# A shorter opening for a two-layer pair kernel: four-step prelude, batches by size, an earlier code exchange on GpSimd, small operations on ScalarE

## The chip, the cores and the metric

The kernel runs on one core of a Trainium2 chip. A core has a matrix engine (TensorE, PE in the profile; its weight loads are listed apart as PEld), a vector engine (VectorE, DVE), a scalar engine (ScalarE, ACT), a general engine (GpSimd, POOL) and a queue engine that issues most transfers (SyncE, SP). Each works through its own list of instructions in order; semaphores order them among each other. Transfers between the chip's memory (HBM) and on-chip memory (SBUF) run on 16 DMA engines. TensorE writes to PSUM, which GpSimd does not read.

The metric is device time in microseconds (us), as the median over runs. The "granted clock" is the share of full speed at which TensorE's clock ran.

## What is computed

The input is x, 384 x 384 x 128 in float32. Two layers follow each other (biases are zeros, scales ones, but the kernel treats them as inputs):

```python
# layer 0
z = layernorm(x)                                   # over the 128 channels
left  = (z @ Wl + bl) * sigmoid(z @ Wlg + blg)     # 384 x 384 x 128
right = (z @ Wr + br) * sigmoid(z @ Wrg + brg)
core  = einsum('ikh,jkh->ijh', left, right)
x = x + sigmoid(x @ Wg + bg) * (layernorm(core) @ Wout + bout)
# layer 1, on the new x
left  = x @ W_left + b_left + x @ W_eq + b_eq
rsum  = sum(x @ W_right + b_right, axis=2)
out   = (left * rsum * sigmoid(x @ W_gate + b_gate)) @ W_out + b_out
return layernorm(out + x)
```

## The kernel before, in words

It works in three phases. Phase 1 makes left and right for all positions and stores them to a scratch tensor, lr_d. Phase 2 multiplies them into core, one channel h at a time (L580). Phase 3 does the rest by rows. The change touches phase 1 alone.

**Chunks, steps, halves.** Phase 1 has 144 chunks (`chunks`). A chunk holds eight rows i for 128 positions k, that is 128 partitions x 8 x 128 numbers, 512 KB. A chunk is two steps, 288 in all; a step (`n, q`) is four rows, and each step has two halves of two rows. In a half, `back` multiplies two 128 x 128 blocks of x by the 128 x 512 weights `wz` (L367, one matmul a row; a float32 matmul leaves two records in the trace), ScalarE takes the sigmoid of one part (L377, tile sg), and VectorE multiplies it with the other part and with the row's scale into tile lr (L379). PSUM has three buffers for `pr`, each holding one half.

**The layernorm is folded in.** `fold` and `weights` put scale and shift of the layernorm into wz and into the shift: three small operations on GpSimd (L181 to L183) on values loaded at the start, four matmuls (L186, L187), two VectorE operations (L194). What stays for each row is a mean-like term `nd`, subtracted from x ahead of the matmul, and a factor `rs`, the reciprocal root, applied after it. For these, VectorE takes statistics of each row (`stats`, bn_stats, L264), then five small operations for a batch of chunks (`powers`, L276 to L280); GpSimd raises to the power -0.5, one operation for each chunk of the batch (`power`, L287, "pow" below); VectorE finishes `nd` by two or three small operations (`centres`, L297, L298, and L300 for the first eight chunks).

**Shift and transposition.** The matmul needs the channels on the partitions. The first eight chunks (PLAIN) are loaded by position; `shift` subtracts nd on GpSimd (L312), and `front` transposes four blocks on TensorE (L327) and copies them back on ScalarE (L328). All later chunks are loaded a second time from a transposed copy (`load_columns`, L135, tile xc). For these, `store_nd` transposes a batch's nd on TensorE (L342), copies it on ScalarE (L344) and stores it to nd_d (L345); `load_shift` loads one row of it per step (L140, tile bc, four buffers); `shift` broadcasts that row over the partitions on GpSimd (L315) and subtracts (L316). The broadcast needs other GpSimd code than the standard one, fetched by a load_library at step 4 (L447; the standard code comes back six steps before the end).

**The order.** The order of each engine's instructions is that of the program (`seq`). Ahead of the main loop a prelude of AHEAD = 6 steps takes statistics, folds the weights and prepares step 0 (`first_step`). In the main loop, step k emits, in this order: one or two pows (two up to k = 40); the shift for step k + 2; `back` for its first half, `centres`, `front` of step k + 1, powers of the next batch, if no batch is under way, and statistics for a later step; then the same for its second half; then the transfers: store_nd, load_columns, load_shift for step k + 6, loads of x (`fetch`), a slice of lr. At k = 4 the shifts run four steps ahead at once, and then comes load_library. Statistics run ahead of the step by a lead that grows by one step a step, from 7 to LEAD = 25. The small weights of the later phases are loaded at k = 4 and combined at k = 20 and 21 (`late_weights`, `late_products`, with a tile m2 of its own).

**Batches.** The first eight chunks are batches of one. Then follow sizes 1, 1, 2, 2, 2, 2, and 4 from there on.

SP's queue carries, in order, the loads of x, of xc and of bc, and the stores of nd and lr; a transfer also waits for the one eight places ahead of it.

Of the kernel before, what the change touches and what calls it, by code (L numbers as in the profile page):

```python
# [8 lines left out]
F32 = mybir.dt.float32  # L9
# [10 lines left out]
def triangle_then_gated_row_kernel(ctx: ExitStack, tc: tile.TileContext, a: dict, out: bass.AP):  # L20
# [59 lines left out]
    with ExitStack() as ctx2:  # L80
# [16 lines left out]
        with tc.tile_pool(name="p1w", bufs=5, side="right") as wp, \  # L97
# [7 lines left out]
            NQ = XR // 4  # L105
            AHEAD, LEAD = 6, 25
            TURN, FETCH = 9, 6
# [3 lines left out]
            batches, at = [(n, n + 1) for n in range(PLAIN)], PLAIN  # L111
            for size in [1, 1, 2, 2, 2, 2] + [4] * len(chunks):
                if at < len(chunks):
                    batches.append((at, min(at + size, len(chunks))))
                    at = batches[-1][1]
# [44 lines left out]
            make_identity(nc, ident)  # L160

            warm = const([P, 1], "warm")
            seq(nc.scalar.activation(warm, mhalf[:, 0:1], AF.Sigmoid))
# [11 lines left out]
            def fold():  # L175
# [4 lines left out]
                busy(1, 1)  # L180
                seq(nc.gpsimd.tensor_tensor(d, b0, g0, ALU.subtract))  # L181
                seq(nc.gpsimd.tensor_tensor(m1, avg, d.to_broadcast([P, P]), ALU.mult))
                seq(nc.gpsimd.tensor_tensor(g0, g0, g0, ALU.add))  # L183

# [38 lines left out]
            def late_weights():  # L223

                m2 = wp.tile([P, C], F32, tag="m2", name="m2", bufs=1)
                seq(nc.vector.tensor_scalar(m2, avg, go, -0.5, ALU.mult, ALU.mult))

                seq(nc.vector.tensor_add(wleft, wleft, weq))
                seq(nc.vector.tensor_add(bleft, bleft, beq))

                seq(nc.vector.tensor_scalar(lns, lns, -1.0, None, ALU.mult))
                return m2
# [29 lines left out]
            def powers(own, lo, hi):  # L266

                if lo == 0:
                    g = XR * (own[1] - own[0])
                    terms[own] += [sp.tile(s, F32, tag=t, name=t, bufs=c)[:, :g] for t, s, c in  # L270
                                   (("mv", [P, 4 * XR, 2], 1),
                                    ("nd", [P, 4 * XR], 2) if own[0] >= PLAIN else ("nd0", [P, XR], PLAIN),
                                    ("rs", [P, 4 * XR], 7) if own[0] >= PLAIN else ("rs0", [P, XR], PLAIN))]
# [17 lines left out]
            def centres(count):  # L291

                for _ in range(count):
# [5 lines left out]
                    if own[0] < PLAIN:  # L299
                        seq(nc.vector.tensor_scalar(nd, nd, 0.5, None, ALU.mult))  # L300
                    centred.add(own)

            centred = set()
            means = []
# [88 lines left out]
            fetch = {0: [4, 5], 1: [6, 7]}  # L393
            for n in range(PLAIN, len(chunks)):
                fetch.setdefault(max(2 + (n - PLAIN) // 2, n - 7, 2 * n - LEAD - 7), []).append(n)
            nds, columns, shifts = {}, {}, {}
# [14 lines left out]
            for k in range(AHEAD):  # L411
# [10 lines left out]
                elif k == 1:  # L422
                    powers((0, 1), 4, XR)
                    power()
                elif k < AHEAD - 1 and k % NQ == 1:
                    powers(batch[k // NQ], 0, XR)
                    power()
                if k == 1:
                    first_step()
                if k == 2:  # L430
                    shift(*steps[1])
            shifted = 2
            powers((2, 3), 0, XR)
            power()
            waiting = batches[AHEAD // NQ:]
            for k, (n, q) in enumerate(steps):
                early = len(means)
                for _ in range(min(len(pows), 1 if k > 40 else 2)):
                    power()
                early = early if k > 40 else len(means)  # L440
                more = 4 if k in (4, len(steps) - 6) else 1
                while shifted < min(len(steps), k + 2 + more):
                    shift(*steps[shifted])
                    shifted += 1
                if more > 1:
                    lib = library_config.all_libraries[10] if k == 4 else library_config.standard
                    seq(nc.gpsimd.load_library(lib))  # L447
                turned = [b for b in batches[PLAIN:] if NQ * b[0] - (TURN if b[0] >= PLAIN + 4 else TURN - 2) == k]
                for half in range(2):
                    if k == 0:  # L450

                        back(n, q, half, (lambda: front(*steps[1])) if half else None)
                    else:
                        back(n, q, half)
                        if half == 0:
                            centres(early)
                        if half == 0 and k + 1 < len(steps):
                            front(*steps[k + 1])
                    if half == 0 and not means and not pows and waiting and 2 * NQ * waiting[0][1] <= given:
                        own = waiting.pop(0)  # L460
                        powers(own, 0, XR * (own[1] - own[0]))
                    stats_to(2 * (k + min(LEAD, AHEAD + k + 1)) + half + 1)
                if q == NQ - 1:
                    del loaded[n], normed[n], columns[n]
                for b in turned:
                    assert b in centred, (k, b, waiting[:1], pows, means)
                    store_nd(b)
                if q == NQ - 1:
# [482 lines left out]
```

## Time and profile before

| | |
|---|---|
| time, median of 3 runs | 3178.05 us (3177.92 to 3178.09) |
| the profiled execution, its own time | 3176.98 us |
| its span | 3175.2 us |
| granted clock, mean | 0.998 |
| TensorE busy | 3144.1 us |
| VectorE, ScalarE, GpSimd busy | 2452.9, 1811.9, 2384.1 us |
| first L367 matmul | 11.91 us |
| first L580 matmul (phase 2) | 1032.43 us |
| read from and written to HBM | 508.14 MB, 286.36 MB |

The span reaches from the first to the last instruction of the one execution that was profiled; its own time is a little longer. Busy time is the time in which an engine executes instructions. In a timeline, a line gives start, duration, engine, source line, operation, output and input tiles, size, and the count of instructions merged; in brackets stands the idle time of the engine ahead of it and what ended it. In the chain of waits, a line gives start, duration, and what was then on the chain that ended last. The phases can be told by their lines: L367 is phase 1, L580 phase 2.

### The profile page before, as it was taken

What the parts mean: (1) busy time and instruction counts of PE and PEld (TensorE: products, weight loads), DVE (VectorE), ACT (ScalarE), POOL (GpSimd) and SP (SyncE); (2) the same over time, 40 slices, a digit from 0 to 9 for tenths busy, and PEclk for the clock granted to TensorE, in tenths of its full rate; (3) what the DMA queues carried; (4) which work ended last, traced back from release to release, by engine and by line L of the source; (5) the groups of instructions that cost most, each with busy time, mean ns of one, the idle gap of its engine ahead of it and who ended that gap; (6) DMA issues with size and microseconds to landing.
All of it is one profiled execution on the core that took longest, in us unless ns stands there. A gap on an engine that the chain in (4) does not pass through costs nothing.

```text
span 3175.2 us, 44349 instructions
## 1 busy us (share of the span) xinstructions
PE 3144.1 (99%) x11344; PEld 1875.8 (59%) x11344; DVE 2452.9 (77%) x7201; ACT 1811.9 (57%) x3793; POOL 2384.1 (75%) x3045
## 2 busy tenths in 40 slices
PE   8999999999999999999999999999999999999998
PEld 3444444444444666666666666677777777777776
DVE  8878888888875555555555788888888888888998
ACT  4444444444444333433433577777777777777776
POOL 5888888888886666666665587787788888888887
PEclk9999999999999999999999999999999999999999
DMA  4787878878782999999999865666666666666552
GB/s 157 289 326 271 329 297 308 315 288 337 272 327 86 266 283 281 285 282 282 284 282 282 302 229 211 216 225 222 218 223 218 224 217 223 219 220 219 209 209 110
DMA packets 474829, 797.41 MB, mean 251 GB/s; under 512 B 21329, under 2 KB 385297, under 8 KB 458194
## 3 DMA queue, kind: packets, MB, share of 16 engines
q1 hardware_dynamic: 473280, 792.61, 72.7%
q8 instruction: 94, 1.54, 0.2%
q10 hardware_dynamic: 1234, 1.77, 0.2%
q14 instruction: 157, 1.29, 0.1%
q0 software_dynamic: 64, 0.20, 0.0%
HBM read 508.14 MB, written 286.36 MB: 250 GB/s over the span
## 4 chain that ended last, share of the span: by engine, by line
PE 95%; POOL 2%; DVE 1%; issue 1%; DMA 1%; ACT 1%; SPq 0%; ACTq 0%; POOLq 0%; DVEq 0%
PE pr L367 28%; PE pc L580 23%; PE py L750 8%; PE pr L721 8%; PE pg L738 8%; PE pl L739 8%; PE pg L690 8%; PE py L751 4%; POOL rs L287 1%; DVE lr L379 1%; POOL xc L316 0%; DVE st L264 0%; DMA xt<-in_x_nat_dram 0%; POOL bc L315 0%; DMA stage<-in_x_nat_dram 0%
## 5 line engine op out<-in xcount | busy, mean ns | idle before, releaser
L367 PE MATMUL pr<-wz,xc 128*128 128x512 f32 x2176 | 939.9, 592 | 5.0 <-ACT sg L377 4.3
L377 ACT ACTIVATE sg<-pr,rs 128x256 f32<-128x256 f32 x1152 | 483.2, 470 | 522.3 <-ACT sg L377 346.4
L580 PE MATMUL pc<-rr,lrh 128*128 128x384 f32 x2304 | 743.3, 486 | 0.3 <-DVE lr L379 0.3
L367 PEld LDWEIGHTS pr<-wz,xc 128*128 128x128 f32 x2176 | 409.8, 190 | 522.7 <-issue 433.6
L379 DVE SCALAR_TENSOR_TENSOR lr<-pr,rs,sg 128x256 f32<-128x256 f32 x1152 | 502.3, 478 | 197.5 <-ACT sg L377 197.5
L580 PEld LDWEIGHTS pc<-rr,lrh 128*128 128x128 f32 x2304 | 452.0, 196 | 291.8 <-issue 1.1
L785 ACT ACTIVATE py<-py,nm,rs 128x128 f32<-128x128 f32 x1149 | 491.8, 429 | 158.2 <-DVE u L743 80.1
L750 PEld LDWEIGHTS py<-wo,u 128*128 128x128 f32 x2304 | 376.6, 191 | 97.5
L591 DVE TENSOR_TENSOR csum<-csum,ct 128x1152 f32<-128x1152 f32 x127 | 176.2, 1387 | 333.8 <-ACT ct L589 333.8
L750 PE MATMUL py<-wo,u 128*128 128x128 f32 x2304 | 402.1, 275 | 0.0
L589 ACT COPY ct<-pc 128x1152 f32<-128x1152 f32 x127 | 142.2, 1119 | 445.2 <-PE pc L580 439.7
L712 POOL TENSOR_TENSOR cs<-ct,rt 128x384 f32<-128x384 f32 x380 | 378.8, 998 | 7.6 <-PE pr L721 4.1
L820 POOL TENSOR_TENSOR yt<-yt,lnb 128x384 f32<-128x384 f32 x380 | 379.7, 1001 | 2.9 <-DVE yt L814 2.6
L316 POOL TENSOR_TENSOR xc<-xc,bc 128x512 f32<-128x512 f32 x272 | 345.2, 1269 | 23.9
L287 POOL TENSOR_TENSOR rs<-nd,mhalf 128x8 f32<-128x8 f32 (+1 forms) x145 | 235.7, 1628 | 157.4 <-ACT ndt L344 107.3
L765 DVE BATCH_NORM_STATS2 st<-py 128x6 f32<-128x128 f32 x1152 | 266.4, 287 | 88.9 <-PE py L751 86.9
L561 POOL COPY rr<-lrh 128x768 f32<-128x768 f32 x128 | 193.7, 1513 | 165.3 <-DMA lrh<-lr_d 154.3
L751 PE MATMUL py<-ident,x1T 128*128 128x128 f32 x1152 | 314.0, 273 | 0.0
L721 PE MATMUL pr<-cs,wc 128*128 128x384 f32 x768 | 313.5, 490 | 0.0
L738 PE MATMUL pg<-x1T,mat_L_conv_W_gate 128*128 128x384 f32 x768 | 310.7, 486 | 0.9 <-ACT g L741 0.9
L690 PE MATMUL pg<-xt,mat_L_conv_Wg 128*128 128x384 f32 x768 | 310.7, 487 | 0.3 <-ACT ct L604 0.2
L739 PE MATMUL pl<-x1T,mat_L_conv_W_left 128*128 128x384 f32 x768 | 310.5, 486 | 0.0
(125 smaller groups left out, 4284.6 us busy)
## 6 DMA issues: line engine op xcount, KB each, us to landing
lr_d<-lr SPq DMA_DIRECT2D x128, 1024.0 KB
lrh<-lr_d SPq DMA_DIRECT2D x128, 640.0 KB
xt<-in_x_row_dram SPq DMA_DIRECT2D x96, 768.0 KB
ct<-core_d SPq DMA_DIRECT2D x95, 768.0 KB
rt<-rstd_d SPq DMA_DIRECT2D x95, 768.0 KB
out_dram<-yt SPq DMA_DIRECT2D x94, 768.0 KB
core_d<-ct SPq DMA_DIRECT2D x125, 576.0 KB
xt<-in_x_nat_dram SPq DMA_DIRECT2D x136, 512.0 KB
```

Of the source, the lines that this page charges most:

```text
L367: seq(nc.tensor.matmul(pr[:, r, :], lhsT=columns[n][:, 4 * q + 2 * half + r, :], rhs=wz, start=True, stop=True))
L377: seq(nc.scalar.activation(sg[r], pr[:, r, 2 * H:], AF.Sigmoid, scale=rs[r]))
L379: seq(nc.vector.scalar_tensor_tensor(t[:, :, c * XR + r0 + r, :], pr[:, r, :2 * H].rearrange("k (h s) -> k h s", s=2), rs[r], sg[r].rearra ...
L580: seq(nc.tensor.matmul(banks[ib], lhsT=t[:, kb, ib * P:(ib + 1) * P, 0], rhs=rr[:, kb], start=(kb == 0), stop=(kb == NB - 1),))
L690: seq(nc.tensor.matmul(pg[:, :N], lhsT=wg0, rhs=r["xT"], start=True, stop=True))
L721: seq(nc.tensor.matmul(pr[:, :N], lhsT=wc, rhs=r["cs"], start=True, stop=True))
L738: seq(nc.tensor.matmul(pg2[:, :N], lhsT=wgate, rhs=r["x1T"], start=True, stop=True))
L739: seq(nc.tensor.matmul(pl[:, :N], lhsT=wleft, rhs=r["x1T"], start=True, stop=True))
L750: seq(nc.tensor.matmul(py[:, s], lhsT=r["u"][:, s], rhs=r["wo"], start=True, stop=False))
L751: seq(nc.tensor.matmul(py[:, s], lhsT=r["x1T"][:, s], rhs=ident, start=False, stop=True, is_transpose=True))
L785: seq(nc.scalar.activation(py[:, s], py[:, s], AF.Identity, bias=bias, scale=scale))
L820: seq(engine.tensor_tensor(yt, yt, lnbb, ALU.add))
```

## The change

It does five things.

- The code exchange of GpSimd (load_library) moves from step 4 to the place right behind the making of the identity matrix; the block of four shifts ahead of it goes.
- The three small operations of `fold` go from GpSimd to ScalarE as activations.
- The prelude has four steps instead of six. The first step's shift stands directly behind the first pow, and other pows and shifts alternate.
- Batches behind the first ten chunks: seven of two, then fours. Up to three batches of one, two of two, and one of four may be under way at once (`free`, `begin`, with buffers of mv by size); one pow a step everywhere. nd has three buffers instead of two; m2 shares the four buffers of bc.
- The lead of the statistics (`goal`) grows by one step a step up to step 12, from 5 to 17, then by one step in three up to 25. Statistics are split evenly over the halves. The loads of x follow `goal`; store_nd comes two steps behind `centres`, or six steps ahead of need at the latest, instead of nine (seven for the first batches).

```diff
-            AHEAD, LEAD = 6, 25
+            AHEAD, LEAD = 4, 25
...
-            for size in [1, 1, 2, 2, 2, 2] + [4] * len(chunks):
+            for size in [1, 1] + [2] * 7 + [4] * len(chunks):
...
             make_identity(nc, ident)
 
+            seq(nc.gpsimd.load_library(library_config.all_libraries[10]))
...
-                seq(nc.gpsimd.tensor_tensor(d, b0, g0, ALU.subtract))
-                seq(nc.gpsimd.tensor_tensor(m1, avg, d.to_broadcast([P, P]), ALU.mult))
-                seq(nc.gpsimd.tensor_tensor(g0, g0, g0, ALU.add))
+                seq(nc.scalar.activation(d, g0, AF.Identity, bias=b0, scale=-1.0))
+                seq(nc.scalar.activation(m1, avg, AF.Copy, scale=d))
+                seq(nc.scalar.activation(g0, g0, AF.Copy, scale=2.0))
...
-                m2 = wp.tile([P, C], F32, tag="m2", name="m2", bufs=1)
+                m2 = bcp.tile([P, 4 * P], F32, tag="bc", name="m2")[:, :C]
...
-                                   (("mv", [P, 4 * XR, 2], 1),
-                                    ("nd", [P, 4 * XR], 2) if own[0] >= PLAIN else ("nd0", [P, XR], PLAIN),
+                                   ((f"mv{g}", [P, g, 2], {XR: 3, 2 * XR: 2}.get(g, 1)),
+                                    ("nd", [P, 4 * XR], 3) if own[0] >= PLAIN else ("nd0", [P, XR], PLAIN),
...
-                    centred.add(own)
-
-            centred = set()
+                    centred[own] = now[0]
+
+            centred, now = {}, [-1]
+
+            def free(own):
+                flying = {p[0] for p in pows} | {p[0] for p in means}
+                size = own[1] - own[0]
+                return sum(o[1] - o[0] == size for o in flying) < {1: 3, 2: 2}.get(size, 1)
+
...
-            for n in range(PLAIN, len(chunks)):
-                fetch.setdefault(max(2 + (n - PLAIN) // 2, n - 7, 2 * n - LEAD - 7), []).append(n)
...
                 elif k == 1:
                     powers((0, 1), 4, XR)
+                    first_step()
                     power()
-                elif k < AHEAD - 1 and k % NQ == 1:
-                    powers(batch[k // NQ], 0, XR)
+                elif k == 2:
+                    shift(*steps[1])
+                else:
+                    powers((1, 2), 0, XR)
                     power()
-                if k == 1:
-                    first_step()
-                if k == 2:
-                    shift(*steps[1])
             shifted = 2
-            powers((2, 3), 0, XR)
-            power()
             waiting = batches[AHEAD // NQ:]
+            turning = batches[PLAIN:]
+
+            def goal(k):
+
+                return 2 * (k + 1 + min(LEAD, 5 + min(k, 12 + (k - 12) // 3))) if k >= 0 else 2 * AHEAD
+
+            for n in range(PLAIN, len(chunks)):
+                k = 2 + (n - PLAIN) // 2
+                while goal(k) < 2 * NQ * (n - 4):
+                    k += 1
+                fetch.setdefault(k, []).append(n)
+
+            def begin(k):
+
+                while waiting and 2 * NQ * waiting[0][1] <= given and free(waiting[0]):
+                    own = waiting.pop(0)
+                    powers(own, 0, XR * (own[1] - own[0]))
+                    if k > 0:
+                        break
+
             for k, (n, q) in enumerate(steps):
+                now[0] = k
                 early = len(means)
-                for _ in range(min(len(pows), 1 if k > 40 else 2)):
+                for _ in range(min(len(pows), 1)):
                     power()
-                early = early if k > 40 else len(means)
-                more = 4 if k in (4, len(steps) - 6) else 1
-                while shifted < min(len(steps), k + 2 + more):
-                    shift(*steps[shifted])
-                    shifted += 1
-                if more > 1:
-                    lib = library_config.all_libraries[10] if k == 4 else library_config.standard
-                    seq(nc.gpsimd.load_library(lib))
-                turned = [b for b in batches[PLAIN:] if NQ * b[0] - (TURN if b[0] >= PLAIN + 4 else TURN - 2) == k]
+                early = early if k > 6 else len(means)
+                if k > 0:
+                    more = 4 if k == len(steps) - 6 else 1
+                    while shifted < min(len(steps), k + 2 + more):
+                        shift(*steps[shifted])
+                        shifted += 1
+                    if more > 1:
+                        seq(nc.gpsimd.load_library(library_config.standard))
...
                         back(n, q, half, (lambda: front(*steps[1])) if half else None)
+                        if half == 0:
+                            centres(len(means))
+                            shift(*steps[2])
+                            shifted = 3
...
-                    if half == 0 and not means and not pows and waiting and 2 * NQ * waiting[0][1] <= given:
-                        own = waiting.pop(0)
-                        powers(own, 0, XR * (own[1] - own[0]))
-                    stats_to(2 * (k + min(LEAD, AHEAD + k + 1)) + half + 1)
+                    if half == 0 and k > 0:
+                        begin(k)
+                    stats_to((goal(k - 1) + goal(k)) // 2 if half == 0 else goal(k))
+                if k == 0:
+                    begin(k)
+                    power()
...
-                for b in turned:
-                    assert b in centred, (k, b, waiting[:1], pows, means)
-                    store_nd(b)
+                while turning and turning[0] in centred and (
+                        k >= centred[turning[0]] + 2 or NQ * turning[0][0] - 6 <= k):
+                    store_nd(turning.pop(0))
```

## The prediction

> **What bounds the kernel now.** I read the head of the page first, then the chain of waits in order of time, then windows and the timeline of the first 190 us.
>
> ```profile
> PE 3144.1 (99%) x11344; PEld 1875.8 (59%) x11344; DVE 2452.9 (77%) x7201; ACT 1811.9 (57%) x3793; POOL 2384.1 (75%) x3045
> ```
> ```profile
> 42.67 1.69 POOL rs L287
> ...
> 173.26 17.40 PE pr L367 x40
> 190.78 27.66 PE pr L367 x64
> 218.55 27.47 PE pr L367 x64
> 246.13 27.67 PE pr L367 x64
> ```
> ```profile
> 11.91:86.90 74.99, 66.18 (x193) 29.89 (x193) 68.33 (x284) 35.14 (x83) 42.34 (x34) 0.98 0.38 132
> 86.90:190.78 103.88, 99.41 (x240) 43.49 (x241) 81.38 (x281) 47.30 (x117) 80.94 (x71) 1.00 0.84 320
> ```
> TensorE bounds the kernel, so only its idle time can be won. In the chain it runs unbroken from 190.78 us: 64 records of L367 are eight steps (four matmuls each, two records a matmul), 27.58 us from piece to piece, 3.45 us a step. Ahead of that, other engines end the waits. The windows (columns: bounds, length, then PE, PEld, DVE, ACT, POOL busy) cover steps 0 to 15 and what follows. A step with its four transposes takes 3.87 us undisturbed (transposes at 28.60 and 32.47 in the timeline): 16 make 61.9 of the 75.0 us, so 13.1 are lost. From 190.78 to the last L367, 29 such pieces and 40.4 us, lie 244 steps of 288; so 44 are done by then. The 28 from 86.90 need 97, the late products (L241 to L244) 1.0: 5 to 6 of the 103.9 us are lost. That is all this change can reach, with the 11.91 us ahead of the first L367.
>
> ```profile
> 5.75 1.04 POOL L287 TENSOR_TENSOR rs<-nd,mhalf 128x4 f32<-128x4 f32 x1 [0.35 <-DVE nd L280]
> 9.32 1.02 POOL L287 TENSOR_TENSOR rs<-nd,mhalf 128x4 f32<-128x4 f32 x1 [2.53 <-DVE nd L280]
> 10.30 1.19 POOL L312 TENSOR_TENSOR stage<-stage,nd 128x256 f32<-128x256 f32 x2
> ...
> 42.67 1.68 POOL L287 TENSOR_TENSOR rs<-nd,mhalf 128x8 f32<-128x8 f32 x1 [4.76 <-DVE lr L379]
> ```
> ```profile
> 27.11 0.17 DVE L276 TENSOR_TENSOR mv<-st 128x16 f32<-128x16 f32 x1
> ...
> 27.82 1.25 DVE L264 BATCH_NORM_STATS2 st<-stage 128x6 f32<-128x128 f32 x6
> 28.99 0.86 DVE L379 SCALAR_TENSOR_TENSOR lr<-pr,rs,sg 128x256 f32<-128x256 f32 x2
> 29.77 0.48 DVE L264 BATCH_NORM_STATS2 st<-stage 128x6 f32<-128x128 f32 x2
> 30.16 0.86 DVE L379 SCALAR_TENSOR_TENSOR lr<-pr,rs,sg 128x256 f32<-128x256 f32 x2
> 30.93 0.15 DVE L297 TENSOR_TENSOR nd<-nd,rs 128x8 f32<-128x8 f32 x1
> ...
> 31.41 0.17 DVE L276 TENSOR_TENSOR mv<-st 128x16 f32<-128x16 f32 x1
> ```
> Three things are seen. The first shift (10.30) stands behind a second pow (L287 at 9.32), though its own input was ready at 7.4. GpSimd is empty for 4.76 us before 42.67, where L447 exchanges its code; VectorE's L297 waits 2.63 us behind it. And a step costs VectorE 4.30 us (27.11 to 31.41) while it fetches its lead in statistics, more than TensorE's 3.87: five operations of powers 0.71, a pair of L379 0.78, a bn_stats 0.195, the three of centres 0.48.
>
> **The change part by part.** New line numbers are about seven higher; I keep the old ones. "h0", "h1" are a step's two halves.
>
> *The exchange behind the identity.* ident ends at 1.51; with the 4.76 us of the row GpSimd is free at 6.27, against 5.75 for the first pow now: 0.5 us late. The row was taken with no DMA running (0.00 share from 37 to 44 us); now the x loads run (0.99 from 2 us). Bounds: 4.76, and waiting until the loads land (20.24 in the chain) plus 4.76, that is 25.0. I take 4.76: an instruction packet (queue q14) got through between 10 and 20 us with the DMA engines at 1.0, so other queues are served beside the loads. [...]
>
> *Small operations on ScalarE.* Three GpSimd operations (0.19, 0.40, 0.19) become three activations; near rows are 0.20 (warm, 128x1) and 0.25 (L344). Input lands at 4.57, so the products of L186 start at 5.2 to 5.4 against 5.29: nothing. It is covered by wz not being wanted before 7.9; without it GpSimd would take these after 6.27. No second table load stands in ScalarE's order.
>
> *The four-step prelude.* The order is now pow, shift, shift, pow. Pow 6.27 to 7.35, centres to 8.0, shifts 0.60 each, transposes 8.65, copy, first L367 at 9.6 (now 11.91). VectorE is what limits from there: wz, two bn_stats, powers to 9.85, second pow to 10.95, centres 11.5, six bn_stats and powers 13.5, step 0's first pair at 13.5 (now 17.94). Two waits on a pow follow, since only one pair covers it: 14.3 to 15.2, and 19.6 to 20.5, where centres also meet the shift (1 us). Step 1 begins at 18.8, step 2 at 24.3, step 3 at 28.15 (now 21.09, 25.85, 30.16).
>
> *Steps 3 to 8.* Lead still grows a step per step until k = 12: two pairs 1.56, eight bn_stats 1.56, powers and centres 1.19, 4.31 as now. Six steps, one without centres, bring step 9 to 53.4; now it is 60.38, because steps 4 and 5 took 6.44 and 7.02 around the exchange, the pushed block of four shifts and VectorE's waits on their port (L298 at 35.98 and L300 at 36.97 took 0.96 and 0.97 instead of 0.17). These go.
>
> *Step 9 on.* Batches thin out: VectorE's steps 9 to 14 come to 3.47, 4.2, 3.1, 3.8, 2.7, 2.3, mean 3.3 under TensorE's 3.87. TensorE, held by three PSUM buffers, starts step 9 at 48.4 (freed by step 7's second pair) and step 12 at 60.3; step 16 then at 60.3 + 4 x 3.87 + three nd transposes of 0.11 = 76.1, now 86.90: **10.8 us** won.
>
> *Steps 16 to 36.* The lead now grows a third of a step per step. Per three steps VectorE has six pairs 4.68, sixteen bn_stats 3.12, one batch 0.77 + 0.35: 8.9 of 10.35 us; GpSimd three broadcasts and shifts (2.13 each, 114.12 to 116.24) and two pows: 9.7. Both fit. The double pow, behind which L297 waited 2.68 us at 141.69 and TensorE 1.56 at 143.89 (again at 171.07), is gone: a pow per step. Of the 5 us lost here I leave 2.4: m2 now takes a turn in the bc tag, so VectorE waits at the end of step 20 for step 23's shift. GpSimd reaches it two pows and three shifts, 9.7 us, after step 18's powers, which end 2 us into that step: 11.7 us against three steps of 10.35, so 1.3 us, partly under TensorE's lead. The rest is port waits. Won: **2.6 us**.
>
> *SP.* Stores of nd come with the bc load right behind that waits for them; it lands in about 3 us (79.08 to POOL's 83.81 bounds it at 4.7), and the shift that reads it is four steps, 14 us, off. Behind it in the queue are an x load (wanted six steps later or more) and lr stores: nothing; without that cover up to 4.7 us for each of nine batches, spread over queues.
>
> Sum: 10.8 + 2.6 = 13.4 us. Later work is bound by TensorE and moves up whole. The profiled run took 3176.98 for a span of 3175.2; its median neighbours 3178.05, 1.07 more. 3176.98 - 13.4 + 1.07 = **3164.7**, say 3165.
>
> **Rivals.** (a) *Exchange at half speed* beside the loads: 9.5 us, first pow at 11.0, all of the opening 4.7 later, since VectorE stands still behind L297: 3169.4. For it: DMA share 0.99. (b) *Port waits eat it.* In steps 12 to 36 each batch's small operations meet GpSimd:
>
> ```profile
> 74.52 2.04 POOL L312 TENSOR_TENSOR stage<-stage,nd 128x512 f32<-128x512 f32 x2
> 74.59 1.00 DVE L297 TENSOR_TENSOR nd<-nd,rs 128x16 f32<-128x16 f32 x1 [0.24 <-POOL rs L287]
> ```
> This and L298 (0.96) cost 1.6 us more than free (0.15 and 0.17); with one broadcast (0.79) ahead of powers VectorE needs 8.9 + 2.4 = 11.3 per 10.35 us, in eight such stretches 8 us: 3172.7. Against it: 61.15 and 131.95 ran free. [...] (c) *Slower:* the exchange's fetch queues behind the x loads and ends at 25.0. The opening is 18.7 later than summed: 5.3 us more than now, 3183. It turns slower where the exchange ends after 6.27 + 13.4 = 19.7 us. For it: loads fill the DMA engines to 20 us; against it, the instruction packets. [...] (d) *TensorE never stalls again* from 9.6: 9.6 + 61.9 + 97, late products 1.0 and six nd transposes 0.7, make 170.2 against 190.78: 3157.5; the waits at 14.3 and 19.6 speak against it.
>
> **How the numbers follow.** Forecast 0.60 (3160 to 3169), (a) 0.12, (b) 0.10, (c) 0.09, (d) 0.09. No change is within 0.2%, 6.4 us, about what a measurement here can tell. Faster holds the forecast, (d), two thirds of (a) and a third of (b): 0.80; slower is (c), 0.09; the rest 0.11. The range 3159 to 3174 leaves out (c) and most of (d).
>
> **What would show it.** First pow near 6.3 and first L367 near 9.6; no gap of GpSimd near 40; L367 of step 16 (first to read xc) near 76; the unbroken chain from about 80 to 130 us on instead of 190.78; no L297 behind a double pow. Wrong: a first pow after 11, x or bc loads as releasers of VectorE or GpSimd after step 16, or gaps of TensorE beyond 190.

## The result, and the profile after

The changed kernel takes 3167.32 us (median of six runs, 3166.68 to 3168.33); the kernel before, on the same chip, 3177.99 (3177.39 to 3179.78). The ratio is 0.9966, 95% interval 0.9954 to 0.9979: faster by about 10.7 us, where 13.4 were forecast (3165). The profiled execution took 3168.33, for a span of 3166.2; it is the slowest of the six.

To find where the time came from, four marks are enough, each the start of the first instruction of its kind: GpSimd's first pow, TensorE's first main-loop matmul, its first matmul on a transposed load (step 16, `xc`), and its first matmul of phase 2 (`pc`).

```
                      before   after    forecast
first pow               5.75    9.40      6.27
first main matmul      11.91   13.00      9.6
step 16 (first xc)     86.90   80.44     76.1
phase 2 (first pc)   1032.43 1022.36
```

So 86.90 - 80.44 = 6.5 us were won by step 16 instead of 10.8, and 945.5 - 941.9 = 3.6 us from there to phase 2 instead of 2.6. Phase 1 gave 10.1 us in all. From phase 2 on nothing changed: from the first pc to the end of the span it is 2142.8 us in the kernel before, 2143.8 in this execution of the changed one, and 2142.6 to 2143.6 in the experiments, whose phase 2 is the same. A microsecond of difference there is one between executions.

The first loss is at the start. The timeline of GpSimd after (start, duration, engine, line, operation, and in brackets the idle time before it and what ended that):

```profile
1.23 0.28 POOL masks.py:199 TENSOR_SCALAR_AFFINE_SELECT ident<-ident 128x128 f32<-128x128 f32 x1 [0.30 <-POOL ident masks.py:197]
9.40 1.05 POOL L288 TENSOR_TENSOR rs<-nd,mhalf 128x4 f32<-128x4 f32 x1 [7.88 <-issue]
11.12 1.19 POOL L319 TENSOR_TENSOR stage<-stage,nd 128x256 f32<-128x256 f32 x2 [0.68 <-DVE nd L301]
13.02 1.01 POOL L288 TENSOR_TENSOR rs<-nd,mhalf 128x4 f32<-128x4 f32 x1 [0.70 <-DVE nd L281]
```

The order is the new one (pow, two shifts, pow), and the shifts no longer stand behind a second pow. But between identity and first pow GpSimd is away for 7.88 us, not 4.76, and "issue" says that no instruction of the profile ended this: it is the exchange of code. The pow's input was ready at 5.5 us. TensorE pays twice: it starts late, and then its clock is low. Its windows after (bounds, length, TensorE busy, granted clock, DMA share, GB/s):

```profile
6.00:8.00 2.00, 1.34 (x7) 1.00 0.99 368
8.00:10.00 2.00, 0.00 (x0) 1.00 1.02 410
10.00:12.00 2.00, 0.20 (x1) 0.82 1.04 424
12.00:14.00 2.00, 2.00 (x5) 0.50 1.02 414
14.00:16.00 2.00, 2.00 (x4) 0.50 1.03 410
16.00:18.00 2.00, 2.00 (x3) 0.50 1.03 410
18.00:20.00 2.00, 2.00 (x8) 0.98 0.95 312
```

It is empty from 7.33 to 11.79 us (4.46 us, ended by the first shift), and the clock granted to it is then half for 6.8 us (0.18 x 2 / 0.5 in the first of these windows, three whole ones, and 0.1 in the last). In the kernel before, TensorE stood empty for 3.45 us and the half clock lasted half as long, 3.4 us (0.65 and 0.50 in the two windows from 12 to 16 us, the rest at 1). The DMA column shows what ran beside the exchange: the x loads at full share.

The end of the opening, in the chain of waits after (start, duration, what):

```profile
100.97 1.28 POOL xc L323
102.62 0.49 PE pw L242 x2
...
103.89 6.97 PE pr L374 x16
110.98 10.30 PE pr L374 x24
121.39 10.40 PE pr L374 x24
```

From 103.89 us on TensorE's work alone makes the chain (before: from 190.78). The last wait ahead of it is that for m2:

```profile
102.27 0.29 DVE L229 TENSOR_SCALAR m<-avg,col_L_conv_onorm_g 128x128 f32<-128x128 f32 x1 [2.03 <-POOL xc L323]
102.62 0.49 PE L242 MATMUL pw<-mat_L_conv_Wout,m 128*128 128x128 f32 x2 [1.06 <-DVE m L229]
```

VectorE stands 2.03 us behind GpSimd's shift of step 23, whose bc buffer m2 takes over, and TensorE 1.06 us behind VectorE.

### The profile page after: what moved, and what is told of

It is laid out like the page before. It is cut to its first block, busy times and chain, and to the rows that moved or that the text cites. A ratio compares the mean times of both kernels' runs of the same rounds, so it can differ in the third digit from the quotient of the medians.

```text
span 3166.2 us, 44409 instructions
## 1 busy us (share of the span) xinstructions
PE 3143.7 (99%) x11345; PEld 1874.5 (59%) x11345; DVE 2449.6 (77%) x7208; ACT 1814.9 (57%) x3797; POOL 2383.5 (75%) x3042
## 4 chain that ended last, share of the span: by engine, by line
PE 97%; DVE 1%; POOL 1%; DMA 0%; ACT 0%; issue 0%; SPq 0%; POOLq 0%; DVEq 0%; ACTq 0%
PE pr L374 30%; PE pc L608 23%; PE py L778 8%; PE pr L749 8%; PE pg L766 8%; PE pl L767 8%; PE pg L718 8%; PE py L779 4%; DMA core_d<-ct 0%; DVE lr L386 0%; DVE st L265 0%; POOL rs L288 0%; PE pq L726 0%; DMA stage<-in_x_nat_dram 0%; PE pt L334 0%
```

## The experiments

All differ from the changed kernel, except where another base is named; line numbers move by one to three between them. Where several were run beside the same runs of the kernel before, their ratios are to those.

**The exchange at step 10.** Is the exchange the loss, and is it cheaper elsewhere?

```diff
             make_identity(nc, ident)
-            seq(nc.gpsimd.load_library(library_config.all_libraries[10]))
...
+                    if k == 10:
+                        seq(nc.gpsimd.load_library(library_config.all_libraries[10]))
```

> The changed kernel with the code exchange moved from behind the identity to step 10, where GpSimd stood idle for 4.47 us (58.99 to 63.47) in the changed kernel's trace. Theory: the exchange beside the x loads (7.88 us from 1.51 to 9.40) is what makes the opening late; without it the first pow starts near 5.5 us, the first L367-type matmul near 9.5, step 16 near 76.5 instead of 80.44, phase 2 near 1018.3 instead of 1022.36, and the time falls by about 4 us to 3163.3. Rival: TensorE's half clock between 11 and 18 us and the second half of chunk 0, which landed at 6.92, hold the opening whatever GpSimd does: less than 1 us won.

3163.38 us (3162.98 to 3165.21), 0.9958 (0.9945 to 0.9970); its slowest run is quicker than the fastest of the changed kernel. First pow at 5.21, first main matmul at 8.54, granted clock 1.00 throughout the opening, step 16 at 76.3, phase 2 at 1018.1. Against this place the one behind the identity costs 80.44 - 76.3 = 4.1 us by step 16, and the time follows. Its own runs of the kernel before were quicker too (3177.10), so set against them the gain is 13.7 us instead of the changed kernel's 10.7. The place isn't free either: the chain of waits here passes through the pow behind the exchange. GpSimd's timeline:

```profile
59.95 1.68 POOL L287 TENSOR_TENSOR rs<-nd,mhalf 128x8 f32<-128x8 f32 x1 [6.00 <-DVE lr L385]
```

The pow's input was ready at 58.3 us, so the exchange took all of the 6.00 us, from 53.95 on. This is no quiet place: the DMA share over these 6.00 us is 0.68. In the three experiments below that also have the exchange at step 10 it took 5.99 to 6.04 us at a share of 0.70 to 0.75.

**The exchange at step 4**, its place in the kernel before, without the block of four shifts beside it (the same edit with `k == 4`).

> The changed kernel with the exchange at step 4 as before the change, but without the block of four shifts ahead of it. Theory: the opening is that of the exchange at step 10, but VectorE waits behind the late pow at steps 4 and 5: 4.76 + 1.64 less 3.1 of cover, 3.3 us, so phase 2 near 1021.6 and the time near 3166.6, about 0.7 us under the changed kernel. Rival: the place at step 4 costs the whole 5.4 us that steps 4 and 5 lost before the change, so the time is near 3168.7, above the changed kernel.

3165.36 us (3164.82 to 3167.20), 0.9965 (0.9951 to 0.9978); step 16 at 78.1, phase 2 at 1020.0. It is nearer to the theory's figure, on its good side. The opening is the quick one (first main matmul at 8.61), but at step 4 VectorE is still the bound, and it waits 1.86 us for the pow behind the exchange, after which one small operation beside a shift takes 1.02 us instead of 0.15: 1.8 us worse at step 16 than with step 10. GpSimd's timeline, and a window in the midst of the exchange (bounds, length, GpSimd busy, granted clock, DMA share, GB/s):

```profile
36.76 1.68 POOL L287 TENSOR_TENSOR rs<-nd,mhalf 128x8 f32<-128x8 f32 x1 [4.83 <-DVE lr L385]
```
```profile
33.00:35.00 2.00, 0.00 (x0) 1.00 0.00 0
```

4.83 us here with DMA share 0.00, 4.76 in the kernel before, also at 0.00. Two experiments ask why it is 7.88 at the start.

**Loads held back.** Chunks 1 to 3 and what follows are loaded only behind the first pow (a small store of its result goes ahead of them in SP's queue); the exchange stays behind the identity.

```diff
-            for n in range(1, 4):
-                load_chunk(n)
...
                     powers((0, 1), 0, 4)
                     power()
+                    seq(nc.sync.dma_start(out=mark_d, in_=terms[0, 1][3][:, 0:4]))
+                    for n2 in range(1, 4):
+                        load_chunk(n2)
```

> The changed kernel with the loads of chunks 1 to 3 (and all behind them in SP's queue) held back by a small store of the first pow's result that SP has to wait for, so that after chunk 0 and the weights (0.77 MB) no load runs beside the exchange. Theory: the x loads lengthen the exchange; it takes near the 4.76 us of the kernel before, and the first pow starts at 6.3 to 6.8 us instead of 9.40. Rival: the first exchange of a program takes some 7.9 us whatever the DMA engines do: 9.4. The time as a whole is not to be read, since the statistics of chunk 1 come late.

The timeline of GpSimd, and windows around it (bounds, length, GpSimd busy, granted clock, DMA share, GB/s):

```profile
7.40 1.05 POOL L287 TENSOR_TENSOR rs<-nd,mhalf 128x4 f32<-128x4 f32 x1 [5.89 <-issue]
```
```profile
1.50:3.50 2.00, 0.01 (x1) 1.00 0.72 232
3.50:5.50 2.00, 0.00 (x0) 1.00 0.44 163
5.50:7.50 2.00, 0.10 (x1) 1.00 0.00 0
```

5.89 us, between the two: the weights and chunk 0 still load for about half of the exchange, and then the DMA engines are empty. The first pow comes at 7.40, neither at 6.3 to 6.8 nor at 9.4, so this run alone doesn't decide. Its time (3169.23, one run) says nothing on the exchange: VectorE waits 3.64 us for chunk 1.

**The exchange between the first shifts and the second pow**, some 9 us in, beside full loads, and at no other place (with m2 early, see below).

```diff
                     powers((0, 1), 4, XR)
                     first_step()
+                    seq(nc.gpsimd.load_library(library_config.all_libraries[10]))
                     power()
```

> The kernel with both edits, and the exchange put into the prelude, between the two first shifts and the second pow of GpSimd: some 8 us in, with the x loads filling the DMA engines until about 20 us. It is not meant as a faster kernel; it tells what stretched the exchange behind the identity. Theory (the x loads beside it): GpSimd's idle time between the end of the shifts, near 8.5 us, and the second pow is 7.7 to 8.8 us, as it was behind the identity, and the second pow starts at 16 to 17.5 us. Rival (the exchange is long only when it is the first thing after the start, loads or not): 4.8 us as at steps 4 and 10, second pow near 13.3 us. The time follows the pow: 3163.4 plus 7 to 8 us by the theory, plus 4 by the rival.

GpSimd's timeline, and windows of GpSimd with the columns as above:

```profile
7.75 1.19 POOL L318 TENSOR_TENSOR stage<-stage,nd 128x256 f32<-128x256 f32 x2 [1.16 <-DVE nd L300]
16.32 1.05 POOL L287 TENSOR_TENSOR rs<-nd,mhalf 128x4 f32<-128x4 f32 x1 [7.37 <-DMA xt<-in_x_nat_dram]
```
```profile
10.00:12.00 2.00, 0.00 (x0) 1.00 1.03 422
12.00:14.00 2.00, 0.00 (x0) 1.00 1.02 412
14.00:16.00 2.00, 0.00 (x0) 0.92 1.03 412
```

The pow's input was ready at 9.6 us, so all of the 7.37 us is the exchange; the load named as releaser has nothing to do with the pow. That is short of the 7.7 to 8.8 expected, and far from the rival's 4.8. So it isn't the start of the program that makes an exchange long; it is long beside the loads. The runs together say the same: 4.76 and 4.83 us at a DMA share of 0.00 over the exchange, 5.89 at 0.39, 5.99 to 6.04 at 0.68 to 0.75, 7.37 to 8.82 at 0.9 to 1.03. The single time of this kernel is 3169.38, 5.9 us above the kernel with both edits, where 7 to 8 were expected.

**m2 ahead of the load.** m2 takes its bc buffer before step 26's load instead of after it, so that it no longer waits for step 23's shift.

```diff
+                if k == 20:
+                    m2 = late_weights()
                 for m, mq in steps[k + FETCH:k + FETCH + 1]:
...
-                if k == 20:
-                    m2 = late_weights()
```

> The changed kernel with m2 made ahead of the bc load of step 20 instead of behind it, so that it takes the slot of step 22's row, whose shift is done, and not that of step 23. Theory: VectorE's wait of 2.03 us at 102.27 and TensorE's of 1.06 at 102.62 go, and phase 2 starts 1.0 us earlier, 3166.3. Rival: the wait is covered by TensorE's lead or only moves to the bc load on SP: no difference.

3166.35 us (3166.23 to 3167.50), 0.9967 (0.9954 to 0.9979). The median is where the theory had it, but that shows nothing: the spread of the runs is as large, and against its own runs of the kernel before (3177.10) the gain is 10.75 us, as good as the 10.67 of the changed kernel. In the trace the gap ahead of the late products is gone; from step 16 to phase 2 it takes 941.2 us instead of 941.9: 0.7, not the 1.0 of the gap.

**TensorE kept busy.** Five matmuls of 512 columns into an unused PSUM tile at the end of the fold; they add work.

```diff
                     seq(nc.tensor.matmul(p[:, gs], lhsT=avg, rhs=brow[:, gs], start=False, stop=True))
+                spare = pps.tile([P, 2, 4 * H], F32, tag="pr", name="spare")
+                for _ in range(5):
+                    seq(nc.tensor.matmul(spare[:, 0], lhsT=avg, rhs=avg.unsqueeze(1).to_broadcast([P, 4, P]), start=True, stop=True))
```

> The changed kernel with five more matmuls of 512 columns behind the fold, into a spare buffer, so that TensorE is busy from 7.3 to about 11.6 us. Theory: the clock of 0.5 from 12 to 18 us comes from the idle 4.46 us ahead of it and costs VectorE its waits of 1.07 and 0.74 us on the sigmoids (17.69 and 20.56); the clock stays at 1.0 and phase 2 starts 1.8 us earlier, 3165.5. Rival: VectorE is held there by pows and its own order, so less than 0.5 us.

3166.72 us (3165.81 to 3167.29), 0.9967 (0.9954 to 0.9979): by its time, the rival. The windows of TensorE (busy, clock, DMA share, GB/s) say something else:

```profile
10.00:12.00 2.00, 1.94 (x6) 1.00 1.03 422
12.00:14.00 2.00, 1.86 (x7) 1.00 1.02 412
...
102.00:104.00 2.00, 2.00 (x10) 0.87 1.00 416
104.00:106.00 2.00, 2.00 (x3) 0.50 1.05 429
106.00:108.00 2.00, 2.00 (x5) 0.77 0.99 412
```
```profile
102.03 0.67 PE pw L248 x6
102.70 8.67 PE pr L377 x16
```

The opening keeps its clock, and step 16 starts at 79.2, 1.2 us earlier than in the changed kernel; the exchange was 0.2 shorter in this execution, so the half clock cost the profiled execution of the changed kernel 1.0 us. But behind the wait for m2 the clock is halved in this execution, and two steps take 8.67 us (last fence, the chain of waits) instead of 6.97: 1.7 us are gone again. The execution with the loads held back shows the same 8.67; the changed kernel and those with the exchange at steps 4 and 10 have the same gap and keep their clock.

The 1.0 us isn't paid in every execution either. In the profile with m2 early TensorE stood empty for 5.02 us, longer than the 4.46 of the changed kernel, and its half clock lasted only 3.4 us (windows of TensorE):

```profile
12.00:14.00 2.00, 1.34 (x5) 0.68 1.04 418
14.00:16.00 2.00, 2.00 (x3) 0.50 1.02 406
16.00:18.00 2.00, 2.00 (x8) 0.97 1.03 410
```

There step 16 came 80.34 - 10.26 = 70.1 us behind the first pow, as here with the clock kept (79.24 - 9.19), where the profile of the changed kernel has 71.0. The profile of the growing lead (below) is like it: empty for 4.70 us, 3.4 us of half clock, 70.1 us. It cost nothing there: VectorE waits 0.37 us for a sigmoid (at 17.86) and 0.51 for the next pow (at 19.24), and with the clock kept 0.96 for that pow.

**The exchange and ScalarE's fold without the rest**: the kernel before with these two alone, and no block of four shifts at step 4.

```diff
+            seq(nc.gpsimd.load_library(library_config.all_libraries[10]))
...
-                more = 4 if k in (4, len(steps) - 6) else 1
+                more = 4 if k == len(steps) - 6 else 1
...
-                    lib = library_config.all_libraries[10] if k == 4 else library_config.standard
-                    seq(nc.gpsimd.load_library(lib))
+                    seq(nc.gpsimd.load_library(library_config.standard))
...
-                seq(nc.gpsimd.tensor_tensor(d, b0, g0, ALU.subtract))
+                seq(nc.scalar.activation(d, g0, AF.Identity, bias=b0, scale=-1.0))
...
```

> The kernel before, with one part of the change alone: the exchange behind the identity, without the block of shifts at step 4, and the three small operations on ScalarE. Theory: the first pow starts at 9.4 instead of 5.75, which costs 3.6 us, and the 5.4 us that steps 4 and 5 lost are won: 1.8 us faster, near 3176.2. Rival: what steps 4 and 5 lost was VectorE's own backlog and comes back later: 2 to 4 us slower than before, 3180 to 3182.

3176.22 us (3175.46 to 3179.03), 0.9996 (0.9987 to 1.0004): no difference that can be told. The exchange took 8.68 us, first main matmul at 16.65, phase 2 at 1031.7, 0.8 earlier than before: what is saved at steps 4 and 5 is spent at the start. So these two by themselves bring next to nothing, and nearly all of the gain needs the rest: prelude, lead, pows and batches.

**A lead that keeps growing by a step per step**, as in the kernel before, beyond step 12.

```diff
-                return 2 * (k + 1 + min(LEAD, 5 + min(k, 12 + (k - 12) // 3))) if k >= 0 else 2 * AHEAD
+                return 2 * (k + 1 + min(LEAD, 5 + k)) if k >= 0 else 2 * AHEAD
```

> The changed kernel with the lead of the statistics growing one step a step up to 25, as before the change, instead of one in three from step 12. Theory: GpSimd then has a pow and a broadcast with shift every step from 14 to 20, 3.77 us against TensorE's 3.45, and VectorE 3.7: phase 2 starts about 2 us later, 3169.3. Rival: the slack is enough and the shape of the lead is worth nothing.

3173.79 us (3172.48 to 3177.96), 0.9988 (0.9980 to 0.9997): 6.5 us dearer than the changed kernel, three times what was expected (5.3 in the traces, where this one is of the quickest run). Step 16 starts at 80.1, near the 80.4 there; all is lost behind it (phase 2 at 1027.7). TensorE in the timeline:

```profile
91.44 3.67 PE L374 MATMUL pr<-wz,xc 128*128 128x512 f32 x8 [0.32 <-DVE lr L386]
95.76 3.67 PE L374 MATMUL pr<-wz,xc 128*128 128x512 f32 x8 [0.54 <-ACT sg L384]
99.75 3.67 PE L374 MATMUL pr<-wz,xc 128*128 128x512 f32 x8 [0.32 <-DVE lr L386]
106.54 0.49 PE L242 MATMUL pw<-mat_L_conv_Wout,m 128*128 128x128 f32 x2 [3.01 <-DVE m L229]
```

Three things add up. VectorE becomes the bound (busy 26.05 of the 28.00 us from 80 to 108), so each step waits 0.3 to 0.5 us; the wait for m2 grows from 1.06 to 3.01; and behind it the clock is halved, so that the next 16 records take 8.67 instead of 6.97 us. The expectation held the first alone. The third, 1.7 us, comes in some executions and not in others, as above.

**Two pows a step**, as the kernel before allowed until step 40.

```diff
-                for _ in range(min(len(pows), 1)):
+                for _ in range(min(len(pows), 1 if k > 40 else 2)):
                     power()
-                early = early if k > 6 else len(means)
+                early = early if k > 40 else len(means)
```

> The changed kernel with two pows a step up to step 40 and the centres in the same step as the second pow, both as before the change. Theory: VectorE waits behind the second pow, about 1.1 us a batch of two and 2 us for each batch of four begun ahead of step 40, part of it within VectorE's slack: phase 2 starts 2 to 6 us later, 3169 to 3173. Rival: the lead hides it, and only the batch sizes mattered: less than 1 us.

3170.84 us (3169.84 to 3172.70), 0.9979 (0.9970 to 0.9988). Double pows are back in the chain of waits:

```profile
63.62 3.23 POOL rs L288 x2
66.86 2.00 POOL stage L319 x2
...
153.82 3.21 POOL rs L288 x2
159.26 3.67 PE pr L374 x8
```

Step 16 comes at 82.9, phase 2 at 1026.1, 3.7 us later than in the changed kernel. The exchange was 0.9 longer in this execution (8.82), but that has nearly vanished by step 3, whose first products start at 32.38 us against 32.26 there: the changed kernel had by then lost nearly as much to its clock. So a pow a step is worth some 3.6 us, 2.4 by step 16 and the rest behind it.

**Both edits**: exchange at step 10 and m2 early.

> After with two edits: the code exchange moved from behind the identity to step 10, and the late weights' m2 made ahead of the next load into the bc buffers instead of behind it. Theory (each was a wait of its own, so the gains add): first xc-reading matmul of step 16 at 76.3 us as with the exchange at step 10 alone, no gap of TensorE ahead of the late products near 98 to 100 us, first phase-2 matmul 1.0 us earlier than 1018.1, so near 1017.2, and 3162.4. Rival: the m2 gap is only the place where another shortage shows, which moves on when it is closed: first phase-2 matmul stays at 1018.1, 3163.4.

3163.51 us (3162.82 to 3165.84), 0.9957 (0.9944 to 0.9969). Its profile starts 0.4 us later than that with step 10 alone (first pow at 5.63, since its input came later; step 16 at 76.7), and from there to phase 2 takes 941.2 instead of 941.8. So the gap is closed, but 0.6 us is less than these medians can tell, and part of the wait moves on, as the rival said: the late weights now crowd VectorE, and TensorE waits for its products (timeline of TensorE).

```profile
104.41 1.96 PE L373 MATMUL pr<-wz,xc 128*128 128x512 f32 x4 [0.33 <-DVE lr L385]
```

**Both edits, and the fold on GpSimd** (the three operations as they were in the kernel before).

> The kernel with both edits, and the fold's three small operations back on GpSimd. With the exchange out of the opening GpSimd waits for the fold's input until 4.57 us anyway, and its three operations take until 5.4 us, so theory: first pow at 5.75 as in the kernel before instead of 5.2, everything in the opening 0.5 us later, first xc matmul near 76.8, 3162.9. The move to ScalarE is then worth half a microsecond with this exchange, and it was worth nothing with the exchange at the start, whose end sets the first pow. Rival: VectorE's queue hides it, first xc matmul stays at 76.3, same time.

3163.34 us (3163.21 to 3164.57), 0.9956 (0.9943 to 0.9968). First pow at 5.69 as expected, but with the fold on ScalarE it was 5.63 in the run beside it; step 16 at 76.8 and 76.7. On GpSimd the fold ends (5.15 + 0.19 = 5.34) before the pow's input is there. The half microsecond expected isn't there: the rival held. With the exchange behind the identity the fold on GpSimd was not tried; there it would stand behind the 7.88 us.

**Both edits, and the old order of GpSimd's prelude** (pow, pow, shifts).

```diff
+                    power()
                     first_step()
-                    power()
```

> The kernel with both edits, and GpSimd's second pow put ahead of the two first shifts again, as in the kernel before. Theory: the first shifts start behind the second pow (near 10 us instead of 6.9), first transposes near 11.2 instead of 7.6, first matmul of the main loop near 12 instead of 8.5, VectorE's first pair of products of step 0 about 2 us later than 12.46 because it stands behind the sigmoid, and an idle stretch of TensorE of some 3.5 us from 7.7, which can halve the granted clock as in after (1 us more). First xc matmul 78.3 to 79.3, 3164.4 to 3165.4. Rival: VectorE's own order sets step 0 (its powers end at 12.4 us in any case), so the order of GpSimd's work is worth less than 0.5 us: 3162.4 to 3162.9.

3165.80 us (3165.02 to 3166.28), 0.9962 (0.9948 to 0.9976). The timeline of TensorE, and two of its windows:

```profile
10.76 1.01 PE L333 MATMUL pt<-ident,stage 128*128 128x128 f32 x4 [3.37 <-POOL stage L318]
```
```profile
12.00:14.00 2.00, 2.00 (x3) 0.50 1.04 420
14.00:16.00 2.00, 2.00 (x4) 0.67 1.01 401
```

Step 16 at 79.3, 2.7 us later than with the new order, phase 2 at 1020.5, and the clock halved: as the theory had it, the time 0.4 above its upper end.

## Why the prediction was right, and where it was not

The sign and the range (3159 to 3174) held; the sum of 13.4 us was 2.7 to 3.3 too large, by the medians or by phase 1. That it was not further off is in part luck: by step 16 the profiled execution was 4.3 us late, and behind it 1.0 us more was won than summed. Step by step:

*What bounds the kernel.* Right. All that was won lies ahead of phase 2, and the rest moved up whole.

*The exchange behind the identity.* This step failed: "I take 4.76: an instruction packet got through between 10 and 20 us with the DMA engines at 1.0, so other queues are served beside the loads." That a packet gets through doesn't say how late. Where no DMA ran the exchange took 4.76 and 4.83 us. Behind the identity it took 7.67 to 8.82 in six profiles with the loads as they are (7.88 in that of the changed kernel), 7.37 in mid-load, 5.99 to 6.04 at step 10 beside fewer loads, and 5.89 where the loads end early. So the first pow came 3.1 us later than summed. Rival (a) had the lengthening beside the loads, with 9.5 us; the 7.88 us lie nearer to it than to the forecast's 4.76. Rival (c), a fetch that waits until the loads land, is excluded: the exchange ends at 9.40 us, and the loads keep the DMA share at 1.01 or more up to 19 us.

*TensorE's clock.* Not in the sum at all, though the profile before showed windows of 0.65 and 0.50. Behind TensorE's empty stretch of 4.46 us the clock was half for 6.8 us, twice as long as before, and with TensorE kept busy step 16 came 1.0 us earlier. It follows from the late exchange: with the exchange at step 10 the clock stays at 1.00. How long it lasts doesn't follow from the empty stretch: 3.4 us behind 4.70 and 5.02, 6.8 behind 4.46. The half clock's lengths read here are two: before, 1.4 + 2.0 = 3.4 us of the windows from 12 to 16; after, 6.8; behind m2, where it happens, 0.5 + 2.0 + 0.9 = 3.4 (the windows from 102 to 108 above). The clock was halved in each of the seven openings in which TensorE was empty for 3.37 us (the old order of the prelude) to 8.03 us (the kernel before with the exchange behind the identity). It was halved behind a shorter stretch too: in the run with the loads held back TensorE was empty for 2.45 us, up to 9.80, and from about 11.7 the clock was half for 3.4. At m2 the gap is 0.99 to 1.08 us and small products of 1.1 us follow, and two of five profiles with it were halved.

*The four-step prelude.* Right in kind. With the clock kept and the first pow at 9.19, step 16 came at 79.24, that is 70.05 us behind the pow; the forecast had 76.1 - 6.27 = 69.8. The order of GpSimd's pows and shifts alone is worth 2.7 us by step 16, with the half clock that the old one brings. With the exchange at step 10 the two forecast waits on a pow are there, 0.96 us each, up to 14.30 and 19.77 (forecast 15.2 and 20.5); in the changed kernel the slow clock covers the first.

*Steps 3 to 8.* Right: VectorE's first products of the steps start at 32.26, 36.55, 40.85, 45.14 and 49.44 us, 4.30 apart against 4.31 forecast, and the 6.44 and 7.02 of the kernel before are gone.

*Step 9 to 16.* Right once its start is shifted: of the 4.3 us by which step 16 came late in this execution, 3.1 are the exchange and 1.0 the clock.

*Steps 16 to 36.* 3.6 us instead of 2.6. Of the port waits held back in the sum little came (that a port is what holds VectorE there no run shows; the traces show small operations of 0.96 to 1.02 us instead of 0.15 to 0.17 beside a GpSimd operation); the wait for m2 came, as the step said, but as 2.03 us of VectorE and 1.06 of TensorE for 1.3 forecast, and removing it brings 0.6 to 0.7. That the lead slows down and the pows go one by one is what gains: undone, they cost 5.7 us and 1.2 from here to phase 2 (the pows another 2.4 by step 16). That is more than the 3.6 won, so they overlap, or other parts of the change cost something here.

*ScalarE and SP.* Costed at nothing. For the fold, shown with the exchange at step 10 only. For SP's stores, no DMA is named as a releaser of TensorE, VectorE or GpSimd between 80 and 160 us; the 3 us for a bc load to land was the author's estimate, under the 4.7 that bound it in the trace before.

Rival (b), 8 us of waits beside GpSimd, did not come: from 54 to 150 us six of ten L298 took 0.15 to 0.17 us, the others 0.49 to 0.78. Rival (d), no stall at all, fell with the first pow.

What stays open: why the exchange varies by 1.15 us between executions of nearly the same opening and is shorter in mid-load (7.37) than in any of them, and when and for how long the clock is halved. The batch sizes, the several batches under way, the third buffer of nd, the later stores and the shorter prelude as such were not undone one by one, so their shares of the gain aren't known. Whether an exchange can be put where it costs nothing was not tried beyond steps 4 and 10; at step 10 it still costs about 1 us, since step 16 comes 71.1 us behind the first pow there and 70.05 with the exchange at the start and the clock kept.

The quickest version found has the exchange at step 10, with or without m2 early: 3163.4 us, some 4 us under the changed kernel, or 3.0 to 3.5 when each is set against its own runs of the kernel before. The intervals of the two ratios overlap (0.9945 to 0.9970 and 0.9954 to 0.9979); that it is quicker rests on run times that don't overlap (3162.98 to 3165.21 and 3166.68 to 3168.33) and on phase 2 starting 4.3 us earlier in the traces.

## What to carry to other kernels

A duration taken from a quiet place of the trace need not hold where the operation is moved beside full DMA queues: here 4.76 us at a DMA share of 0.00 became 7.88 at 0.90. Look at the DMA share of both places first. When an engine's opening is late, ask what TensorE's idle time does to its clock and add it to the sum: here 3.1 us of lateness brought 1.0 more at step 16 in the profiled execution, and nothing in two others. And give the filler work that reads ahead only the rate at which it stays under the bound engine: here a lead growing a third as fast was worth 5.3 us in the traces, 1.7 of them through the clock.

## What the hardware showed that was not expected

- The code exchange of GpSimd took longer beside loads: 4.76 and 4.83 us at a DMA share of 0.00, 5.89 at 0.39 (the loads end halfway), 5.99 to 6.04 at 0.68 to 0.75, 7.37 to 8.82 at 0.9 to 1.03.
- The clock was halved behind a gap of 1.06 and of 1.08 us and some small products in two profiles, at 1.7 us each time, and not in three others (gaps of 0.99 to 1.07 us). That is as much as the edits which it hides: keeping TensorE busy won 1.0 us by step 16 and lost 1.7 behind m2.
- The length of the half clock in the opening doesn't follow from the empty stretch ahead of it: 3.4 us behind 2.45, 3.37, 3.45, 4.70 and 5.02 us, 6.8 behind 4.46, 4.51 and 8.03.
